# Routing taken out of the queue of second halves, and a norm moved into the scan before it

## The chip, the core and the metric

The kernel runs on one core of a Trainium2 chip. The metric is the device time of one launch in microseconds (us). Engines are called PE (TensorE matmul), PEld (its weight loads), DVE (VectorE), ACT (ScalarE), POOL (GpSimd) and SP (SyncE, which here only issues transfers).

## The reference

One decoder layer over 64 sequences of 128 tokens of width 256, all in float32. It has three parts, each followed by a residual sum and a layer norm:

```python
x = _layernorm(x + mamba(x))            # L0_attn: norm, W_in, conv, silu, selective scan, gate, W_out
x = _layernorm(x + retention(x, ctx))   # L0_xattn: q from x, k and v from ctx, xpos, decay mask
x = _layernorm(x + moe(x))              # L0_ffn: a shared expert, and 2 of 8 routed experts
...
    xn = _layernorm(x, gamma, beta)
    x_inner, z = jnp.split(xn @ W_in, 2, axis=-1)
    x_conv = jax.nn.silu(causal_conv(x_inner))
    xp = x_conv @ W_x                          # B, C (16 states each), delta
    y = _selective_scan(x_conv, A, Bmat, Cmat, softplus(delta))
    return ((y + x_conv * D_skip) * silu(z)) @ W_out + x
...
    probs = sigmoid(x @ router_w.T + routing_bias)
    scores, indices = top_k(probs, 2)          # normed to sum 1
    combined = sum over the two: score * (silu(x @ gate) * (x @ up)) @ down
```

## The kernel before, in words

At run time the kernel picks one of two bodies. With these inputs the decay rows are all alike, so `_shared_decay` runs.

**Groups.** The 64 sequences are 16 groups of 4 (`GB`), so a group has 512 tokens. A group goes through these generators; each `yield` hands control back to a planner, with the number of microseconds of matmul work that should pass before the next step.

- `front` (L632): the norm of x into `xn` (`layernorm`, L577: statistics on DVE, a `pow` on POOL, then `shift` on DVE, then four ACT writes), transposes, the product with `w_in_s`, convolution on DVE (L662), silu, then the products with `w_x_s` for B, C and delta, which go out to DRAM and come back spread over partitions (`bj`, `cj`, `cq`).
- `scan` (L750): the selective scan as matrix products inside each sequence. POOL scales `bj` and `cj` (L754), PE makes sums of the decays (`d`, `dlb`), DVE makes `eq`, `gq` and the mask matrix `mt` (L799), PE transposes `xc` (L806) and multiplies with `mt` (L813), and DVE makes y and the gated `sz` (L817, L820).
- `after` (L824), the second half: product with `w_out_s`, norm, the keys `kh` and values of the context `cT`, queries `qh`, scores, and the second norm, which leaves `x2`.
- `route` (L946): transposes of `x2`, the router's logits, ranks of the experts (`sel`, L985), running counts (`pre`), addresses, and eight indirect stores by POOL (L1028) that scatter the rows of the group to the lists of its experts. For groups in `LATE` (7 to 12) SP then stores `x2` and its transpose as well.
- `early_shared` (L1069): the shared expert, for groups not in `LATE` beside the others, for the rest at the end.

After groups 3, 7, 11 and 15 `tile_list` (L1096) turns the counts into a list of tiles of one expert each. `one_tile` (L1284) does such a tile: its rows and weights are fetched on SP, two products, and an indirect store of the results by POOL.

**The planner.** Several chains run side by side. Each carries a position in units of groups, and the number of microseconds of matmuls until it may go on. `abreast` (L1312) always steps the chain with the lowest position among those that may go on, and jumps its clock ahead when none may. `placed` (L1330) gives a chain its place: `placed(gen, at, length, span)` takes the chain from `at` to `at + span` as `length` microseconds of its own work and waits pass. The chains are: `first_halves` (front and scan of group g from position g-1 on), `second_start` (the same for group 1), `second_halves` (after and route of group g from g+1 on), `shared_ones` (from g+2 on) and `tiles_beside`. What is issued first has priority, but the compiler's scheduler still reorders instructions of an engine where one is ready earlier and its buffer is free.

Gates stand between the chains. The second half of group g begins when g is scanned, and group g-2 has its shared expert added (or, in `LATE`, has been routed). The first half of group g loads the x of g+1 (POOL, L629), and waits until group g-2 has read its x (`read`).

**Buffers.** Most big buffers exist once and are shared by name tags: `xn` and the scan's `eq` are one, `xnT`, `cq` and `xd0` are one, `cT` and `x1T` are one, and so are `qh` and the second copy of the rows to be scattered, `row1`. PSUM has 5 banks `pm` and 3 banks `gu`. Group 1 has buffers of its own in the place of expert weights that are not loaded yet, so that groups 0 and 1 start together.

Of the kernel before, what the change touches and what calls it, by code (L numbers as in the profile page):

```python
# [16 lines left out]
P = 128  # L17
L = 128
D = 256
# [10 lines left out]
GB = 4  # L30
# [481 lines left out]
def _shared_decay(ctx, K):  # L512
# [41 lines left out]
    def buffer(st, shape, name, tag=None):  # L554

        if "own" not in st:
            return one.tile(shape, F32, name=name, tag=tag or name)
        return shaped(st["own"][tag or name], shape)
# [68 lines left out]
    def load_x(g):  # L627
        xt = xts[g % 3]
        nc.gpsimd.dma_start(out=xt, in_=x[g * GB : (g + 1) * GB].rearrange("b l d -> l b d"))  # L629
        return xt  # L630

    def front(st):  # L632


        xt = st["xt"]
        xn = buffer(st, [P, GB, D], "xn", "xn")
        if st is states[0]:
            rstd, shift = K.norm0
            for b in range(GB):
                read_by = nc.scalar.activation(  # L640
                    xn[:, b, :], xt[:, b, :], AF.Identity, bias=shift[:, b : b + 1], scale=rstd[:, b : b + 1]
                )
            first_read.append(read_by.ins.name)
        else:
            yield from layernorm(xn, xt)
        yield 2.6
        xnT = buffer(st, [P, KD, T], "xnT", "xnT")
        transposed(xnT, xn, gam, bet)
        yield 1.2
# [100 lines left out]
    def scan(st):  # L750

        xcf, dl, tok, bj, cj, cq = (st[k] for k in ("xcf", "dl", "tok", "bj", "cj", "cq"))
        for t, h in ((bj, halvesT[0]), (cj, halvesT[1])):
            nc.gpsimd.tensor_tensor(seqs(t), seqs(t), h.unsqueeze(1).to_broadcast([KB, GB, L]), ALU.mult)  # L754

        d1 = little(st, [P, GB, Q], "d1")
        nc.vector.tensor_tensor(
            d1, dl.unsqueeze(2).to_broadcast([P, GB, Q]), place.unsqueeze(1).to_broadcast([P, GB, Q]), ALU.mult
        )
        dlb = little(st, [P, GB, 32], "dlb")  # L760
        nc.vector.tensor_copy(dlb, dl.unsqueeze(2).to_broadcast([P, GB, 32]))
        yield 4.4 if fetched[0] else 2.4
        pin = pm.tile([P, GB, Q], F32, name="pm")
        product(pin.rearrange("p b i -> p (b i)"), lhsT=after_in, rhs=d1.rearrange("p b i -> p (b i)"), start=True, stop=True)
        eq = buffer(st, [P, GB, NS, Q], "eq", "xn")
        nc.vector.tensor_tensor(
            eq, pin.unsqueeze(2).to_broadcast([P, GB, NS, Q]),
            a_row.unsqueeze(1).unsqueeze(3).to_broadcast([P, GB, NS, Q]), ALU.mult,
        )
        pof = pm.tile([KB, T], F32, name="pm")  # L770
        for b in range(GB):
            for q in range(4):
                product(
                    pof[32 * q : 32 * q + 32, b * L : (b + 1) * L], lhsT=dlb[:, b, :], rhs=middle[min(q, 2)],
                    start=True, stop=True, tile_position=(0, 32 * q),
                )
        eb = buffer(st, [KB, T], "eb", "bcs")
        nc.scalar.activation(eb, pof, AF.Exp, scale=a_col)
        nc.scalar.activation(eq, eq, AF.Exp)
        nc.vector.tensor_tensor(bj, bj, eb, ALU.mult)  # L780
        nc.vector.tensor_tensor(cj, cj, eb, ALU.mult)
        yield 4.2
        pmt = pm.tile([P, GB, L], F32, name="pm")
        for b in range(GB):
            product(
                pmt[:, b, :], lhsT=bj[:, b * L : (b + 1) * L], rhs=cj[:, b * L : (b + 1) * L], start=True, stop=True
            )
        nc.vector.tensor_tensor(eq, eq, cq, ALU.mult)
        nc.vector.tensor_tensor(
            eq, eq, tok[:, :, 0:NS].unsqueeze(3).to_broadcast([P, GB, NS, Q]), ALU.mult  # L790
        )
        gq = little(st, [P, GB, Q], "gq")
        nc.vector.tensor_reduce(gq, eq.rearrange("p b n i -> p b i n"), AX.X, ALU.add)
        mt = buffer(st, [P, GB, NQ, Q], "mt", "dm")
        nc.vector.tensor_tensor(
            mt, gq.unsqueeze(2).to_broadcast([P, GB, NQ, Q]), causal.unsqueeze(1).to_broadcast([P, GB, NQ, Q]), ALU.mult
        )
        mtf = mt.rearrange("p b j i -> p b (j i)")
        nc.vector.tensor_tensor(mtf, mtf, pmt, ALU.add)  # L799
        yield  # L800

        xd = [buffer(st, [P, 2, DI], f"xd{j}", tag) for j, tag in enumerate(("xnT", "xd"))]
        for b in range(GB):
            ps = pm.tile([P, DI], F32, name="pm")
            for c in range(CI):
                turn(ps[:, c * P : (c + 1) * P], xcf[:, c, b * L : (b + 1) * L], ident)  # L806
            nc.scalar.activation(xd[b // 2][:, b % 2, :], ps, AF.Copy, scale=dl[:, b : b + 1])  # L807
            yield 0.5 if b < GB - 1 else 3.6
        acc = st["sz"]
        for c in range(CI):  # L810
            ps = pm.tile([P, GB, L], F32, name="pm")
            for b in range(GB):
                product(  # L813
                    ps[:, b, :], lhsT=xd[b // 2][:, b % 2, c * P : (c + 1) * P], rhs=mtf[:, b, :], start=True, stop=True
                )
            y = xcf[:, c, :]
            nc.vector.scalar_tensor_tensor(  # L817
                y, xcf[:, c, :], dsk[:, c : c + 1], ps.rearrange("p b l -> p (b l)"), ALU.mult, ALU.add
            )
            nc.vector.tensor_tensor(acc[:, c, :], acc[:, c, :], y, ALU.mult)  # L820
            yield 0.5 if c < CI - 1 or not fetched[0] else 2.0
        st["acc"] = acc
# [489 lines left out]
    def abreast(*chains):  # L1312

        alive = [[gen, whole, 0.0, 0.0] for gen, whole in chains]
        while any(c[1] for c in alive):
            able = [c for c in alive if c[3] <= work[0]]
            if not able:
                work[0] = min(c[3] for c in alive)  # L1320
                continue
            c = min(able, key=lambda c: c[2])
            try:
                c[2], wait = next(c[0])
            except StopIteration:
                alive.remove(c)
                continue
            c[3] = work[0] + wait

    def placed(gen, at, length, span=1.0):  # L1330

        passed = 0.0
        while True:
            before = work[0]
            try:
                wait = next(gen) or 0.0
            except StopIteration:
                return
            passed += work[0] - before + wait
            yield at + span * min(1.0, passed / length), wait  # L1340
# [2 lines left out]
        yield from front(st)  # L1343
        yield from scan(st)

    def second_half(g, st):
        yield from after(g, st)
        yield 2.6
        yield from route(g, st)
        for k, (groups, *_) in enumerate(BATCHES):  # L1350
            if groups == g + 1:
                tile_list(k)
                refill()
# [142 lines left out]
    def until(ready, at):  # L1496
        while not ready():
            yield at, 0.5

    def first_halves():  # L1500
        states[2]["xt"] = load_x(2)
        yield from placed(start, 0.0, 54.0)
        states[0]["scanned"] = True
        for g in range(2, NG):
            if g + 1 < NG:
                yield from until(lambda: "read" in states[g - 2], g - 1)
                states[g + 1]["xt"] = load_x(g + 1)
            yield from placed(first_half(states[g]), g - 1, 54.0)
            states[g]["scanned"] = True

    def second_start():
        yield from placed(first_half(states[1]), 0.2, 54.0)
        states[1]["scanned"] = True

    def second_halves():
        for g in range(NG):
            yield from until(lambda: "scanned" in states[g] and (g < 2 or "added" in states[g - 2]), g + 1)
            yield from placed(second_half(g, states[g]), g + 1, 60.0)
            states[g]["routed"] = True
            if g in LATE:  # L1520
                states[g]["added"] = True
# [10 lines left out]
    def tiles_beside():  # L1532

        for at, length in places:
            if at >= NG + 1:
                return
            i = listed[0]
            while i == known[0]:
                yield at, 1.0
            yield from placed(one_tile(), at, 11.0, length)  # L1540

    abreast((first_halves(), True), (second_start(), True), (second_halves(), True), (shared_ones(), True), (tiles_beside(), True))
    chains.close()


# [291 lines left out]
```

## Time and profile before

| | |
|---|---|
| median of three runs | 1954.57 us (1946.59 to 1956.8) |
| profiled execution | 1935.52 us, span 1933.7 us |
| mean granted clock of PE | 0.988 |
| PE busy | 1866.0 us, 97% of the span |
| DVE busy | 971.9 us, 50% |
| ACT busy | 748.7 us, 39% |
| POOL busy | 473.1 us, 24% |
| groups 2 to 6 without or with few expert tiles | until about 435 us |
| expert tiles alone | about 1545 to 1790 us |
| last sums and stores | from about 1790 us |

The profile shows one execution. For every engine it has the busy time, and for the waits which instruction ended them. A fraction of the full TensorE clock is shown for each stretch: at 0.50 a matmul takes twice as long. Matmul ends are modelled, so a busy PE can still be below its peak. Line numbers are those of the kernel before.

### The profile page before, as it was taken

How to read it: one execution, taken by the hardware profiler on the slowest of the kernel's cores; microseconds unless marked ns; L12 is line 12 of the kernel's file. 1: busy time of each engine (PE TensorE's matmuls, PEld its weight loads, DVE VectorE, ACT ScalarE, POOL GpSimd, SP SyncE). 2: the span in 40 equal slices, each digit the busy share in tenths (PEclk: the TensorE clock that was granted, in tenths of full speed). 3: DMA queues.
4: the chain of work that ended last, by engine and by line, in shares of the span. 5: the costliest groups of instructions: out<-in, count | busy, mean ns of one | idle time of the engine just before them, and what ended most of it. 6: DMA issues, size and time to landing. Idle time of an engine off the chain costs nothing.

```text
span 1933.7 us, 26599 instructions
## 1 busy us (share of the span) xinstructions
PE 1866.0 (97%) x9252; PEld 1393.1 (72%) x9252; DVE 971.9 (50%) x2409; ACT 748.7 (39%) x1238; POOL 473.1 (24%) x715
## 2 busy tenths in 40 slices
PE   7799999999999998999999999999999999999997
PEld 3656656668686856787877768786877888999554
DVE  5766667745455557455555474554333111111774
ACT  5553553443434343535353544352231222222233
POOL 2102212303030403132322313141313322222111
PEclk9999999999999998999999999999999999999998
DMA  4211211423150214323242224232204443353782
GB/s 142 53 35 44 68 49 41 137 85 95 45 153 28 85 35 153 101 77 113 64 133 93 79 93 123 61 123 92 81 19 128 146 150 118 120 175 107 276 305 89
DMA packets 101352, 199.10 MB, mean 103 GB/s; under 512 B 22904, under 2 KB 61432, under 8 KB 96600
## 3 DMA queue, kind: packets, MB, share of 16 engines
q1 hardware_dynamic: 80952, 144.24, 23.6%
q0 software_dynamic: 17328, 51.41, 7.8%
q10 hardware_dynamic: 2928, 1.65, 0.3%
q8 instruction: 75, 1.23, 0.3%
q14 instruction: 69, 0.57, 0.1%
HBM read 206.81 MB, written 58.08 MB: 137 GB/s over the span
## 4 chain that ended last, share of the span: by engine, by line
PE 72%; DVE 3%; issue 3%; DMA 2%; ACT 2%; POOL 2%; SPq 0%; POOLq 0%; ACTq 0%; DVEq 0%
PE pm L545 37%; PE gu L545 32%; PE pm L549 4%; DMA picked<-ys 1%; POOL rstd L588 1%; DMA ys<-rows_out,to 1%; DVE st L583 0%; DVE x L1305 0%; DMA cq<-chunks 0%; POOL xs L1028 0%; ACT x L593 0%; ACT xn L593 0%; DVE hc L1051 0%; DVE xt L1305 0%; ACT xc L667 0%
## 5 line engine op out<-in xcount | busy, mean ns | idle before, releaser
L545 PE MATMUL gu<-rows_T,routed_gu 128*128 128x256 f32 (+1 forms) x2496 | 499.4, 351 | 1.5 <-ACT rows_T L1232 1.5
L545 PEld LDWEIGHTS gu<-rows_T,routed_gu 128*128 128x128 f32 x2496 | 417.7, 191 | 59.2 <-issue 14.2
L1261 DVE TENSOR_TENSOR hid<-hid,gu 128x512 f32<-128x512 f32 x135 | 92.7, 687 | 394.8 <-PE gu L545 344.4
L545 PE MATMUL pm<-routed_d,hid 128*128 128x256 f32 x1080 | 252.7, 381 | 0.0
L545 PE MATMUL gu<-x2T,shared_w 128*128 128x512 f32 x512 | 232.0, 596 | 4.4 <-DVE hc L1051 3.3
L545 PE MATMUL pm<-xnT,w_in_s 128*128 128x512 f32 x480 | 226.6, 599 | 1.7 <-ACT xnT L606 1.1
L545 PEld LDWEIGHTS pm<-routed_d,hid 128*128 128x128 f32 x1080 | 199.7, 190 | 29.6 <-issue 5.4
L1277 POOL DMA_INDIRECT ys<-rows_out,to x135 | 135.0, 1000 | 331.4 <-ACT rows_out L1276 282.8
L545 PEld LDWEIGHTS gu<-x2T,shared_w 128*128 128x128 f32 x512 | 94.3, 190 | 112.1 <-issue 93.6
L593 ACT ACTIVATE x<-x,shift,rstd 128x256 f32<-128x256 f32 x156 | 82.3, 590 | 232.5 <-DVE shift L590 222.2
L588 POOL TENSOR_TENSOR rstd<-var,mhalf 128x4 f32<-128x4 f32 (+1 forms) x69 | 72.8, 1055 | 370.6 <-DVE var L586 318.6
L662 DVE SCALAR_TENSOR_TENSOR xc<-pm,cw,xc 128x508 f32<-128x508 f32 (+1 forms) x180 | 131.4, 738 | 37.2 <-ACT xc L657 36.0
L545 PEld LDWEIGHTS pm<-xnT,w_in_s 128*128 128x128 f32 x480 | 90.2, 192 | 80.3 <-issue 72.3
L1276 ACT ACTIVATE rows_out<-pm,wt 128x256 f32<-128x256 f32 x135 | 57.9, 471 | 205.2 <-PE pm L545 185.4
L1260 ACT ACTIVATE hid<-gu 128x512 f32<-128x512 f32 x135 | 80.6, 597 | 110.0 <-PE gu L545 109.7
L545 PE MATMUL pm<-w_out_s,sz 128*128 128x256 f32 x512 | 116.4, 381 | 0.4 <-ACT xd L807 0.2
L545 PEld LDWEIGHTS pm<-w_out_s,sz 128*128 128x128 f32 x512 | 95.4, 191 | 14.3 <-issue 1.0
L657 ACT ACTIVATE xc<-pm,cb,cw 128x512 f32<-128x512 f32 x60 | 46.7, 778 | 144.2 <-PE pm L545 144.2
L1028 POOL DMA_INDIRECT xs<-x,index x64 | 71.6, 1118 | 78.0 <-DVE row L1024 42.8
L583 DVE BATCH_NORM_STATS2 st<-x 128x6 f32<-128x256 f32 x196 | 77.4, 408 | 1.6 <-DMA x<-in_x_dram 0.7
L545 PE MATMUL gu<-shared_w,hc 128*128 128x256 f32 x320 | 72.5, 380 | 0.0
L1051 DVE TENSOR_TENSOR hc<-hc,gu 128x512 f32<-128x512 f32 x64 | 43.5, 680 | 55.2 <-PE gu L545 35.1
(288 smaller groups left out, 2571.2 us busy)
## 6 DMA issues: line engine op xcount, KB each, us to landing
routed_gu<-in_ffn_dram SPq DMA_DIRECT2D x78, 1024.0 KB
routed_d<-in_ffn_dram SPq DMA_DIRECT2D x78, 512.0 KB
picked<-ys SPq DMA_DIRECT2D x16, 1024.0 KB
rows_in<-xs SPq DMA_DIRECT2D x57, 258.0 KB
cT<-in_ctxT_dram POOLq DMA_DIRECT2D x16, 512.0 KB, 4.1
x_rows<-x SPq DMA_DIRECT2D x16, 512.0 KB
cq<-chunks SPq DMA_DIRECT2D x15, 512.0 KB
x<-in_x_dram POOLq DMA_DIRECT2D x9, 512.0 KB, 4.2
```

Source lines behind the costliest of these rows:

```text
L545: nc.tensor.matmul(out, lhsT=lhsT, rhs=rhs, **how)
L549: nc.tensor.transpose(out, src, ident)
L583: nc.vector.bn_stats(st, src[:, b, :])
L588: nc.gpsimd.tensor_tensor(rstd, var, mhalf[:, 0:n], ALU.pow)
L593: nc.scalar.activation(dst[:, b, :], src[:, b, :], AF.Identity, bias=shift[:, b : b + 1], scale=rstd[:, b : b + 1])
L657: nc.scalar.activation(xcf[:, c, :], ps, AF.Identity, bias=cb[:, c : c + 1], scale=cw[:, c, TAPS - 1 : TAPS],)
L662: nc.vector.scalar_tensor_tensor(xc[:, c, :, s:], ps3[:, :, : L - s], cw[:, c, TAPS - 1 - s : TAPS - s], xc[:, c, :, s:], ALU.mult, ALU.add,)
L1028: s = nc.gpsimd.indirect_dma_start(out=xs, in_=rows[k][:, b, :], in_offset=None, out_offset=bass.IndirectOffsetOnAxis(ap=index[:, b, k : k ...
L1260: nc.scalar.activation(hc, psg, AF.Silu)
L1261: nc.vector.tensor_tensor(hc, hc, psu, ALU.mult)
L1276: nc.scalar.activation(y[:, j, :], ps[:, j, :], AF.Copy, scale=wt[:, j : j + 1])
L1277: s = nc.gpsimd.indirect_dma_start(out=ys, in_=y[:, j, :], in_offset=None, out_offset=bass.IndirectOffsetOnAxis(ap=to[:, j : j + 1], axis=0),)
```

## The change

It has two parts. In the first, `scan` of group 0 and of every group from 2 on makes the norm of the next group of `first_halves` (group 2 after group 0, else g+1): statistics, `pow` and `shift` right after `mt`, and the four ACT writes into `xn` after the transposes of `xc`. `front` of that group finds `xn` made and skips its norm and the planned waits of 4.2 and 2.6 behind it. In the second, `route` and the tile lists leave `second_halves` and become a chain `routings` of their own. `after` of group g now goes from g+1 to g+1.6, `routing` of group g from g+1.6 to g+2, and the second half of the next group no longer has to wait for the routing of this one.

```diff
--- before.py
+++ after.py
@@ -633,8 +633,14 @@
 
 
         xt = st["xt"]
-        xn = buffer(st, [P, GB, D], "xn", "xn")
-        if st is states[0]:
+        made = "xn" in st
+        if made:
+            xn = st["xn"]
+        else:
+            xn = buffer(st, [P, GB, D], "xn", "xn")
+        if made:
+            pass
+        elif st is states[0]:
             rstd, shift = K.norm0
             for b in range(GB):
                 read_by = nc.scalar.activation(
@@ -643,7 +649,7 @@
             first_read.append(read_by.ins.name)
         else:
             yield from layernorm(xn, xt)
-        yield 2.6
+        yield 0.0 if made else 2.6
         xnT = buffer(st, [P, KD, T], "xnT", "xnT")
         transposed(xnT, xn, gam, bet)
         yield 1.2
@@ -797,6 +803,13 @@
         )
         mtf = mt.rearrange("p b j i -> p b (j i)")
         nc.vector.tensor_tensor(mtf, mtf, pmt, ALU.add)
+
+        norm = None
+        if "next" in st:
+            then = st["next"]
+            xn = then["xn"] = buffer(then, [P, GB, D], "xn", "xn")
+            norm = layernorm(xn, then["xt"])
+            next(norm)
         yield
 
         xd = [buffer(st, [P, 2, DI], f"xd{j}", tag) for j, tag in enumerate(("xnT", "xd"))]
@@ -806,6 +819,8 @@
                 turn(ps[:, c * P : (c + 1) * P], xcf[:, c, b * L : (b + 1) * L], ident)
             nc.scalar.activation(xd[b // 2][:, b % 2, :], ps, AF.Copy, scale=dl[:, b : b + 1])
             yield 0.5 if b < GB - 1 else 3.6
+        for _ in norm or ():
+            pass
         acc = st["sz"]
         for c in range(CI):
             ps = pm.tile([P, GB, L], F32, name="pm")
@@ -1343,9 +1358,7 @@
         yield from front(st)
         yield from scan(st)
 
-    def second_half(g, st):
-        yield from after(g, st)
-        yield 2.6
+    def routing(g, st):
         yield from route(g, st)
         for k, (groups, *_) in enumerate(BATCHES):
             if groups == g + 1:
@@ -1499,6 +1512,8 @@
 
     def first_halves():
         states[2]["xt"] = load_x(2)
+        for g in (0, *range(2, NG - 1)):
+            states[g]["next"] = states[max(g + 1, 2)]
         yield from placed(start, 0.0, 54.0)
         states[0]["scanned"] = True
         for g in range(2, NG):
@@ -1513,9 +1528,16 @@
         states[1]["scanned"] = True
 
     def second_halves():
+
         for g in range(NG):
             yield from until(lambda: "scanned" in states[g] and (g < 2 or "added" in states[g - 2]), g + 1)
-            yield from placed(second_half(g, states[g]), g + 1, 60.0)
+            yield from placed(after(g, states[g]), g + 1, 38.0, 0.6)
+
+    def routings():
+        for g in range(NG):
+            yield from until(lambda: "x2" in states[g], g + 1.6)
+            yield g + 1.6, 2.6
+            yield from placed(routing(g, states[g]), g + 1.6, 26.0, 0.4)
             states[g]["routed"] = True
             if g in LATE:
                 states[g]["added"] = True
@@ -1539,7 +1561,7 @@
                 yield at, 1.0
             yield from placed(one_tile(), at, 11.0, length)
 
-    abreast((first_halves(), True), (second_start(), True), (second_halves(), True), (shared_ones(), True), (tiles_beside(), True))
+    abreast((first_halves(), True), (second_start(), True), (second_halves(), True), (routings(), True), (shared_ones(), True), (tiles_beside(), True))
     chains.close()
 
 
```

## The prediction

> **What bounds the kernel now.** I read, in this order, the page's busy shares and slices, the PE's waits, the PE's own timeline in the stretches where it waits, the granted clock in windows around those, and the POOL and DVE timelines of one group.
>
> ```profile
> PE 1866.0 (97%) x9252; PEld 1393.1 (72%) x9252; DVE 971.9 (50%) x2409; ACT 748.7 (39%) x1238; POOL 473.1 (24%) x715
> ...
> PE   7799999999999998999999999999999999999997
> ...
> PEclk9999999999999998999999999999999999999998
> ```
>
> The first row says that TensorE is busy for all but 1933.7 - 1866.0 = 67.7 us. The change touches no matmul, so nothing but this idle time and the time lost to a lowered clock can be won. The slices show where it lies: at the start, at the end, and in one slice in the middle (the sixteenth, 8 in both rows). By windows: 13.9 us idle before 48 us, about 24 us from 48 to 435 us, nothing from 435 to 720 us, 8.0 us from 725 to 773 us, about 3 us from there to 1545 us, and 18 us after 1790 us. The end (late sums, loads of picked rows) is not touched.
>
> ```profile
> PE pm L549 <- ACT xn L593: 8.8, 10, 2.0
> ...
> PE pm L545 <- DVE cj L781: 4.6, 3, 2.3
> PE pm L545 <- DVE sel L985: 4.5, 2, 2.8
> ...
> PE pm L545 <- DVE dlb L761: 3.1, 2, 2.9
> ```
>
> Columns: total us, times, longest. The largest wait is for `xn`, the norm at the head of the first half; `sel` is the router's. Two single rows of the PE timeline, one of each kind (the bracket is the idle time before it):
>
> ```profile
> 141.50 0.63 PE L545 MATMUL pm<-sel,upto 128*128 128x32 f32 x2 [2.78 <-DVE sel L985]
> ```
> ```profile
> 313.43 0.33 PE L549 MATMUL pm<-ident,xn 128*128 128x128 f32 x1 [1.48 <-ACT xn L593]
> ```
>
> And the gap in the middle, where group 7 is routed beside group 9's scan:
>
> ```profile
> 724.52 0.38 PE L549 MATMUL pm<-ident,bcs 128*128 128x128 f32 x2
> 726.67 0.41 PE L545 MATMUL pm<-sel,upto 128*128 128x32 f32 x2 [1.77 <-DVE sel L985]
> 727.36 0.41 PE L545 MATMUL pm<-pre,ones 128*128 128x32 f32 x2 [0.28 <-DVE pre L991]
> 730.63 0.66 PE L545 MATMUL pm<-d,after_in 128*128 128x64 f32 x2 [2.86 <-DVE dlb L761]
> 731.22 1.94 PE L545 MATMUL pm<-middle,dlb 128*32 128x128 f32 x32
> 735.47 2.04 PE L545 MATMUL pm<-cj,bj 128*128 128x128 f32 x8 [2.31 <-DVE cj L781]
> ```
> ```profile
> 725.00:730.00 5.00, 0.82 (x4) 0.59 (x4) 4.71 (x25) 3.18 (x5) 1.26 (x1) 0.78 0.53 177
> 730.00:735.00 5.00, 2.52 (x34) 1.89 (x34) 3.30 (x13) 1.63 (x2) 2.60 (x3) 0.50 0.48 138
> 735.00:740.00 5.00, 4.54 (x21) 4.57 (x22) 4.08 (x4) 1.37 (x2) 4.08 (x4) 0.50 0.23 82
> ```
>
> Columns of the windows: us, busy PE, PEld, DVE, ACT, POOL, granted clock, DMA share, GB/s. The clock drops to 0.50 after the gap, so what the PE then does takes twice its time: the gap costs more than itself.
>
> **The norm moved (edit 1).** Removed from the head of `front`: the layernorm call and the planner's waits of 4.2 and 2.6; added in `scan` of the group before: the same instructions. They are 4 bn_stats (0.40 us), 4 aggregates (0.17), `var`, `shift` (0.16 each) on DVE, one `pow` (1.05) on POOL and four ACT writes (2.08 together). No DMA moves: the load of x is still issued one group ahead (301.71 us for a norm that would now come some 60 us later; 4.2 us to landing), past nothing new. Group 0 prepares group 2, then each its next; group 1 keeps its own norm.
>
> What goes: the PE's waits for `xn` by its timeline are 2.02 (group 2), 1.23, 1.63, 1.64 and 2.15 us (group 6), 8.7 in all. After group 6 tiles of the experts hide the norm already, and there I cost the gain at nothing. Two of the gaps carried the clock down: 0.56 and 0.87 in the 3 us windows from 96 and 99 us (3 x 0.44 + 3 x 0.13 = 1.7 us), 0.50 and 0.95 from 390 and 393 us (1.5 + 0.15 = 1.65 us). At most 8.7 + 1.7 + 1.65 = 12.0 us.
>
> Here the Trainium skill speaks another way. "TensorE: Matmul & The Clock Gate", Part 1, says that the clock falls to half after an idle window of about 3.4 us; by it no gap of 2 us costs clock, and the edit would bring 8.7 us. The rows show 0.56 after a gap of 2.02 us (with a 0.3 to 0.5 us trickle of work behind it). I take the rows, 12.0.
>
> What it may cost: the DVE work is the same in sum, but now comes in one step with `mt`, ahead of the four y updates (0.74 + 0.69 us each) that free the PSUM banks. From 291 to 313 us DVE idles only about 3 us, so 4 x (0.32 + 0.09) + 0.3 = 1.9 us put first are 1.9 us late for what follows. In the trace of before, the stats of xt stood in the same stretch (304.17 to 311.22 us), behind the y updates; they leave there what they take earlier. Bounds: nothing, if they slip into DVE's idle time before the scan (263 to 275 us is nearly empty), or 1.9 us in each of the five groups without tiles, 9.5 us. I take 3 us, nearer the lower end, as five PSUM banks stand between. ACT is idle from 292 to 305 us, where its four writes would go: nothing; without that hole they would hold the next evacuation 2.1 us.
>
> **Routing as its own chain (edit 2).** Routing no longer stands in the queue of second halves: `after(g+1)` need not wait for `route(g)` and its planned waits (1.0 + 0.6 + 2.2 + 4.6 or 7.6 + 0.4 + 3.0 + 5.0 + 5.0). The positions hardly move: attention's own length is 21.6 of matmuls plus 12 of waits, some 34; 34/60 = 0.57 before and 0.6 x 34/38 = 0.54 now, routing starts at 0.60 both times and ends near 1.0. So the order stays where chains are plentiful, and only where all others wait can `after(g+1)` step in. It is still gated: it needs group g+1 scanned, and group g-1's shared expert added. Two places qualify.
>
> At 141.5 us (group 0 routed, no gate for group 1): 2.78 us of gap, and the clock at 0.50 for 141 to 147 us and 0.91 for the next three, (2.5 + 3.0) x 0.5 + 0.27 = 3.0 us. In all 5.8. The DVE is full there (3.00 of 3.00 us from 138 to 141 us), so I take half, 2.9.
>
> At 724.9 us: group 6's shared expert has just ended (724.5 us), group 8 is scanned, and its w_out products follow only at 741.0 us behind the tile list: 2 x 3.6 us of matmuls that depend on nothing still running. The gaps are 1.77 + 0.28 + 2.86 + 2.31 = 7.2 us; the clock costs 0.82 x 0.22 + 2.52 x 0.5 + 4.54 x 0.5 + 5.0 x 0.15 (0.85 from 740 us) = 4.5 us. Together 11.7. What is late next: the work drawn forward is missing at 741 to 763 us, before the first tile, but the next first half, ready without its norm, has 14 us of w_in products for that. I take 8 us.
>
> The queues that routing is moved past: on POOL its 8 indirect stores, 0.96 + 0.30 us each:
>
> ```profile
> 297.34 0.96 POOL L1028 DMA_INDIRECT xs<-row,index  x1 [0.30 <-issue]
> 301.71 0.81 POOL L629 DMA_DIRECT2D x<-in_x_dram  x1 [3.42 <-DVE x L841]
> 304.35 1.05 POOL L588 TENSOR_TENSOR rstd<-var,mhalf 128x4 f32<-128x4 f32 x1 [1.82 <-DVE var L586]
> ```
>
> They run from 287.09 to 298.30 us; the attention's `pow` comes 6 us after the last. On SP: two stores of x2 for groups 7 to 12 and the fetches behind the tile list; attention issues nothing on SP, so no order changes there. `row1` lies in the place of `qh`, so the next `qh` (DVE, some 316 us) waits for the last of these stores (298.3 + 2.6 to landing = 301): 15 us of slack, which an earlier attention eats into. The load of cT, on POOL, is issued 55 us before its use (318.9 for 374 us). Cost between nothing and one scatter row, 10 us, in each of the two places; I take 1 us each, as before the slack was 6 and 15 us.
>
> **Sum.** 12.0 - 3.0 + 2.9 + 8.0 - 2.0 = 17.9, say 18 us. The profiled execution took 1935.5 us (span 1933.7), and would take 1917.5, 0.93% less. The median of the three runs, 1954.6, stands 1.0% above the profiled one; 0.93% off it is 1936.4 us.
>
> **Rivals.**
> *Hidden anyway (same).* Other waits take the place of the `xn` ones: each group still shows 0.8 us for `mt`, and `xnT` and the y updates now follow each other closely. If those give back the 8.7 us and the gap at 725 us stays since `after(8)` isn't let in, 3 us remain: 1951 us. For it: PE waits of 0.2 to 0.8 us stand everywhere behind the larger ones. Against: from 415 us on the PE idles nowhere, whenever it has a choice of work.
>
> *The early norm caught behind the stores (slower).* The `shift` of the norm sits in DVE's in-order queue right after `mt`, and waits for a `pow` in POOL's queue. The 8 stores of routing take 10.1 us there. In before `mt` came at 294.4 us, inside their run of 287 to 298 us. If the `pow` comes behind the stores, DVE stands up to 10 us with the y updates, the residuals and the experts' products queued behind it. Taking 4 us of stall (half a row left, less a little) in 13 groups, 52 us, of which half comes through to the PE past its five banks, 26 us, against some 12 won: 14 slower, 1969 us. It decides from about 2 us of stall in each group (13 us on the PE). Against: by position the norm (0.65 of the group) precedes the stores (0.83), and the stats can go early. For: the planner counts matmuls, not POOL's microseconds.
>
> *All of it (faster still).* Everything above at its full size, 12.0 + 5.8 + 11.7 = 29.5 us: 1925 us.
>
> *It doesn't do what it says:* for group 1 it surely doesn't; for the others the norm may be drawn ahead or held, but the head of `front` loses its wait either way.
>
> **How the numbers follow.** About 0.5% (10 us) is what a measurement can tell from no change. My sum and "all of it" have 0.56 together (0.46 and 0.10), hidden anyway 0.23, caught behind the stores 0.21. The likeliest case alone spans 1925 to 1944. The range goes on to 1968: half the slower case, and 1920 below for a little beyond the full size; some 0.17 are left out.
>
> **What would show it.** Right: the wait PE <- ACT `xn` is gone or under 1 us; w_out products of group 8 stand between 725 and 735 us and the clock stays at 1.00 there; 50 to 435 us loses 10 us or more of idle time; the end is as before. Wrong: `shift` waiting on POOL for well over its present 61.7 us in total (0.93 each), with PE waits for `xc` (L817) or `xnT` new in the list; or the gap of the sixteenth slice still there.

## The result and the profile after

The changed kernel takes 1960.22 us (median of 20 runs, 1955.83 to 1964.78), the kernel before 1948.70 us (20 runs, 1944.93 to 1958.89): a ratio of 1.0054 with the interval [1.0044, 1.0065]. It is slower by 0.54%, some 10.5 us by the ratio, where 0.93% faster was forecast. The two profiled executions stand further apart, 1935.52 and 1962.05 us, since the one of before was among its fastest. So times are compared by ratios below, each against runs of the kernel before on the same chip, and the traces are read for where waits stand, not for the last microseconds.

The page of the changed kernel, its first two parts:

```profile
PE 1874.3 (96%) x9252; PEld 1400.2 (71%) x9252; DVE 985.4 (50%) x2409; ACT 761.6 (39%) x1248; POOL 466.0 (24%) x715
...
PE   7889998899999998999999999999999999999997
...
PEclk9899999899999998999999999999999999999998
```

The span is 1960.3 us. The number of matmuls is unchanged, but PE now idles 1960.3 - 1874.3 = 86.0 us (67.7 before), and is busy 8.3 us longer for the same work: that is lowered clock (mean 0.982, 0.988 before). The slices show new dips near the start: the third, seventh and eighth in the row of PE, the second and eighth in that of the clock. What PE waits for (total us, times, longest):

```profile
PE pm L545 <- DVE qh L875: 12.0, 2, 7.0
PE pm L545 <- DVE dlb L767: 10.6, 2, 7.6
...
PE pm L549 <- ACT xn L646: 5.5, 1, 5.5
PE pm L545 <- DVE cj L787: 5.3, 2, 3.1
PE pm L545 <- ACT xnT L606: 4.8, 3, 2.1
```

The waits for the norm of later groups (ACT `xn`, L593 before, 8.8 us in 10) are gone; L646 is the first group's own start, as long as it was before. But `qh` is new, and `dlb` and `xnT` have grown (3.1 and 1.1 us before). Two rows of DVE's waits go with them:

```profile
DVE shift L590 <- POOL rstd L588: 92.7, 65, 5.8
...
DVE qh L873 <- DMA xs<-row,index: 12.1, 2, 7.4
```

and the first of these in the kernel before:

```profile
DVE shift L590 <- POOL rstd L588: 61.7, 66, 2.4
```

The `shift` of the norms waits 31 us more in all for POOL's `pow`. A wait of about 1 us is the `pow` itself; 18 of the 65 waits are now longer than 1.6 us, where 2 of 66 were. And `qh`, which lies in the place of `row1`, now waits for routing's last stores, which it never did in the trace of before.

Most of the new idle time lies early. The stretch from 50 to 440 us, first after, then before (us, busy PE, PEld, DVE, ACT, POOL, granted clock, DMA share, GB/s):

```profile
50.00:440.00 390.00, 352.46 (x1742) 239.42 (x1740) 250.81 (x614) 171.01 (x262) 71.23 (x79) 0.94 0.21 62
```
```profile
50.00:440.00 390.00, 365.51 (x1805) 243.53 (x1805) 262.84 (x639) 184.22 (x279) 79.11 (x83) 0.97 0.21 64
```

PE idles 37.5 us there instead of 24.5, at a lower clock, where at least 10 us less was to be seen. The gap at 725 us, in the same columns:

```profile
725.00:730.00 5.00, 5.00 (x21) 3.66 (x20) 3.58 (x12) 2.23 (x2) 1.52 (x2) 1.00 0.08 26
730.00:735.00 5.00, 5.00 (x20) 3.52 (x19) 0.14 (x2) 1.47 (x3) 3.78 (x5) 1.00 0.58 206
735.00:740.00 5.00, 5.00 (x21) 3.79 (x20) 0.65 (x2) 0.60 (x1) 2.41 (x3) 1.00 0.24 87
...
765.00:770.00 5.00, 2.44 (x21) 2.04 (x19) 5.00 (x7) 2.53 (x4) 1.17 (x3) 0.93 0.96 375
770.00:775.00 5.00, 3.31 (x14) 3.06 (x14) 2.92 (x4) 2.08 (x4) 0.00 (x0) 0.50 0.48 165
```

It is closed, at full clock, as forecast, but not by the work that was forecast. Products of the shared expert, of the next first half and of expert tiles fill it; the w_out products of group 8 come only behind it:

```profile
736.36 3.62 PE L545 MATMUL pm<-w_out_s,sz 128*128 128x256 f32 x16
```

A new gap stands 40 us later, where PE waits for `qh` (3.3 us) and the clock is 0.50 again.

### The profile page after: what moved, and what is told of

Read it like the earlier page. It is cut to its first block, busy times and chain, and to the rows that moved or that the text cites. A ratio compares the mean times of both kernels' runs of the same rounds, so it can differ in the third digit from the quotient of the medians.

```text
span 1960.3 us, 26607 instructions
## 1 busy us (share of the span) xinstructions
PE 1874.3 (96%) x9252; PEld 1400.2 (71%) x9252; DVE 985.4 (50%) x2409; ACT 761.6 (39%) x1248; POOL 466.0 (24%) x715
## 5 line engine op out<-in xcount | busy, mean ns | idle before, releaser
L545 PEld LDWEIGHTS pm<-routed_d,hid 128*128 128x128 f32 x1080 | 202.0, 192 | 35.3 <-issue 10.3
L593 ACT ACTIVATE x<-x,shift,rstd 128x256 f32<-128x256 f32 x156 | 82.8, 591 | 115.2 <-DVE shift L590 112.0
L1043 POOL DMA_INDIRECT xs<-x,index x64 | 63.6, 993 | 121.0 <-DVE row L1039 83.9
L1247 ACT COPY rows_T<-pm 128x512 f32<-128x512 f32 (+1 forms) x78 | 41.1, 528 | 123.2 <-PE pm L549 95.6
```

The costliest lines, as they stand in the source:

```text
L545: nc.tensor.matmul(out, lhsT=lhsT, rhs=rhs, **how)
L593: nc.scalar.activation(dst[:, b, :], src[:, b, :], AF.Identity, bias=shift[:, b : b + 1], scale=rstd[:, b : b + 1])
L1043: s = nc.gpsimd.indirect_dma_start(out=xs, in_=rows[k][:, b, :], in_offset=None, out_offset=bass.IndirectOffsetOnAxis(ap=index[:, b, k : k ...
```

## The experiments

The kernels are arranged by the question that they answer. Where an expectation gives theories letters, a letter stands for the cause that is named with it. Every ratio is to the kernel before on the same chip.

### Each part alone

**The early norm alone**: routing goes back into the queue of second halves.

```diff
-    def routing(g, st):
+    def second_half(g, st):
+        yield from after(g, st)
+        yield 2.6
         yield from route(g, st)
...
-            yield from placed(after(g, states[g]), g + 1, 38.0, 0.6)
-
-    def routings():
-        for g in range(NG):
-            yield from until(lambda: "x2" in states[g], g + 1.6)
-            yield g + 1.6, 2.6
-            yield from placed(routing(g, states[g]), g + 1.6, 26.0, 0.4)
+            yield from placed(second_half(g, states[g]), g + 1, 60.0)
...
```

> The early norm alone; routing stays in the queue of second halves. Theory A (the routing chain is what costs: the next attention runs into routing's row1 and its late stores): 5 to 12 us below the kernel before (1937 to 1944), no PE wait for xn after group 1, and PE waits for qh under 1 us. Theory B (the early norm costs, by DVE work ahead of the y updates and shift behind other POOL work): 5 to 15 us above before, with PE waits behind dlb, xnT or xc. Theory C (only the changed order of the matmuls and the clock after gaps count, either edit does it): within 5 us of before.

Measured: 1975.99 us, a ratio of 1.0155 [1.0142, 1.0168]. The part that was to win is the one that costs most. PE's longest list entry is now

```profile
PE pm L545 <- ACT xnT L606: 24.3, 8, 5.3
```

and one of the eight waits can be followed through four engines. The timelines of POOL, DVE, ACT and PE in the same 15 us (start, us, engine, line, operation, and in the bracket the idle time before it and its releaser):

```profile
157.20 0.96 POOL L1043 DMA_INDIRECT xs<-row,index  x1 [0.31 <-issue]
158.46 0.96 POOL L1043 DMA_INDIRECT xs<-row,index  x1 [0.30 <-issue]
159.42 0.82 POOL L629 DMA_DIRECT2D x<-in_x_dram  x1
160.25 1.08 POOL L588 TENSOR_TENSOR rstd<-var,mhalf 128x4 f32<-128x4 f32 x1
```
```profile
156.03 0.17 DVE L586 TENSOR_SCALAR var<-mv 128x4 f32<-128x4 f32 x1
156.11 0.68 DVE L873 TENSOR_TENSOR kh<-pm,rot_s 128x512 f32<-128x512 f32 x1
161.37 0.16 DVE L590 SCALAR_TENSOR_TENSOR shift<-mv,rstd 128x4 f32<-128x4 f32 x1 [4.58 <-POOL rstd L588]
```
```profile
161.57 1.58 ACT L593 ACTIVATE x<-x,shift,rstd 128x256 f32<-128x256 f32 x3 [16.42 <-DVE shift L590]
163.06 1.42 ACT L606 ACTIVATE xnT<-pm,bet,gam 128x512 f32<-128x512 f32 x2
```
```profile
158.41 1.02 PE L545 MATMUL gu<-x2T,shared_w 128*128 128x512 f32 x2
163.87 3.78 PE L545 MATMUL pm<-xnT,w_in_s 128*128 128x512 f32 x4 [4.44 <-ACT xnT L606]
```

`var` is ready at 156.2 us, but its `pow` stands behind the last of routing's eight stores (149.42 to 159.42 us) and a load, and starts at 160.25. DVE's queue stops at `shift` for 4.58 us. ACT's queue stops at the three writes of x1 that need `shift`, and the evacuation `xnT`, which needs nothing of this norm, stands behind them. PE waits 4.44 us for `xnT`, and then its four matmuls take 3.78 us, where four of the same take 1.88 us at 172.15 us: the granted clock is 0.50 from 164 to 168 us. The same meeting comes four times between 160 and 410 us. DVE stalls 4.58, 4.50, 4.51 and 4.03 us in them, and PE waits 4.44, 4.36, 4.37 and 5.27 us, 18.4 of the 24.3 us. The norm that is caught is not the early one. It is the norm of x1 in the second half that runs beside it.

**Routing as its own chain alone**: the early norm is dropped, so that `front` makes its norm and waits as before.

```diff
-        for g in (0, *range(2, NG - 1)):
-            states[g]["next"] = states[max(g + 1, 2)]
```

> Routing as its own chain alone; every norm stays at the head of front. Theory A: 10 to 20 us above before (1959 to 1969), since the xn waits of 8 us are back as well, with PE waits for qh of 5 us or more. Theory B: 3 to 12 us below before, the gap at 725 us filled. Theory C: 0 to 10 us above.

Measured: 1949.29 us, 1.0019 [1.0012, 1.0026]: a small loss, where 8.9 us were to be won. Two windows of this kernel, the columns as above:

```profile
660.00:800.00 140.00, 132.76 (x715) 100.80 (x714) 90.42 (x241) 63.52 (x103) 34.76 (x47) 0.98 0.36 110
800.00:1460.00 660.00, 644.23 (x3264) 492.05 (x3263) 347.82 (x821) 273.70 (x447) 167.58 (x229) 1.00 0.27 85
```

and the same two of the kernel before:

```profile
660.00:800.00 140.00, 131.80 (x600) 92.23 (x599) 84.97 (x216) 54.85 (x89) 28.86 (x37) 0.95 0.25 84
800.00:1460.00 660.00, 656.95 (x3385) 511.83 (x3384) 338.47 (x843) 269.58 (x448) 174.59 (x239) 1.00 0.29 90
```

The first stretch holds the routing of group 7 and what follows it in both kernels. Here that routing comes 30 us earlier (`sel` at 696 us instead of 726), and its gap comes with it: PE idles 5.7 us between 695 and 710 us. Over the whole stretch the chain saves 132.76 - 131.80 = 1.0 us of idle time and, by the clock of 0.98 instead of 0.95, some 4 us more, where 8.0 were forecast. In the second, in which the trace of before had nearly no idle time, PE loses 656.95 - 644.23 = 12.7 us. There attention of one group, routing of another and expert tiles now overlap, and a `pow` meets other work on POOL. One such meeting, in three lines of POOL, one of DVE and one of PE:

```profile
860.64 1.04 POOL L1292 DMA_INDIRECT ys<-rows_out,to  x1 [0.15 <-issue]
861.99 0.97 POOL L1292 DMA_INDIRECT ys<-rows_out,to  x1 [0.30 <-issue]
862.99 1.05 POOL L588 TENSOR_TENSOR rstd<-var,mhalf 128x4 f32<-128x4 f32 x1
```
```profile
864.07 1.23 DVE L590 SCALAR_TENSOR_TENSOR shift<-mv,rstd 128x4 f32<-128x4 f32 x1 [4.69 <-POOL rstd L588]
```
```profile
865.70 0.43 PE L545 MATMUL pm<-d,after_in 128*128 128x64 f32 x2 [1.11 <-DVE d L763]
```

`shift` again, this time behind the scaling of `bj` and two stores of tile results; the scan's `d` stands behind it in DVE's queue, and PE waits for that.

### What of the early norm costs: the norm, the waits, or POOL

**The early norm with the planned waits kept**: the norm is made in the scan, and `front` still lets the planner count 4.2 and 2.6 us of matmuls before its transposes.

```diff
         if made:
-            pass
+            yield 4.2
...
-        yield 0.0 if made else 2.6
+        yield 2.6
```

> The early norm alone, but front keeps the planner's waits of 4.2 and 2.6 us that the edit had taken out, though nothing is left to wait for; instructions as in the early norm alone (1976 us). Theory D (the loss is the lost lead: with 6.8 us of planned waits gone, each first half runs that much ahead, so the second half's norm meets routing's eight stores on POOL): the waits for xnT of 4.4 us go, and the time falls by 20 to 30 us, to within 5 us of before. Theory B (the norm's own work on DVE and ACT at its new place): still 20 us or more above before.

Measured: 1920.46 us, 0.9924 [0.9911, 0.9937]. The same norm in the same place, and with two waits of the planner put back a gain of 0.76% stands where a loss of 1.55% was. PE idles 58.0 us (span 1917.2, busy 1859.2) instead of 96.0, the clock is 0.990 instead of 0.981. The waits of DVE and the place on POOL that answers to the one above:

```profile
DVE shift L590 <- POOL rstd L588: 59.0, 65, 2.6
```
```profile
155.65 0.96 POOL L1043 DMA_INDIRECT xs<-row,index  x1 [0.30 <-issue]
156.63 0.81 POOL L629 DMA_DIRECT2D x<-in_x_dram  x1
157.62 1.04 POOL L588 TENSOR_TENSOR rstd<-var,mhalf 128x4 f32<-128x4 f32 x1 [0.19 <-DVE var L586]
```

The `pow` still comes right after stores and load, but now POOL waits 0.19 us for `var`: the norm comes just after the stores, where without the waits it came 4 us too early. The planned waits did not only bridge the norm. They also set how far the first half runs ahead of routing, and with it where the second half's norm falls.

**Half of the waits kept**: only 3.4 of the 6.8 us.

```diff
-        yield 0.0 if made else 2.6
+        yield 3.4 if made else 2.6
```

> The early norm alone with a planned wait of 3.4 us at the head of front: half of the 6.8 us kept. If the loss grows with the lead: between the kernels with all and with none of it, ratio 1.000 to 1.008. If it is a collision that either happens or not: near 0.992 or near 1.015.

Measured: 1.007 [1.0052, 1.0087] (1963.57 us). `shift` waits 69.5 us, the longest 4.4; `xnT` 5.0 us in 5. It lies between 0.9924 and 1.0155 in time and in waits, but the single stall is not smaller. Of the four early stalls of `shift` one is left, at 163.59 us and 4.43 us long; the other three are gone, and two of 3.5 and 3.7 us stand in other places. A meeting happens or it does not, and half the lead brings fewer of them. PE's waits for `xnT` explain only 3.9 of the 28 us between 0.9924 and 1.007; where the rest comes from was not traced.

**The root of the x1 norm off POOL**: the early norm alone once more, without planned waits; only the `pow` of the norm of x1 is replaced, by a root on ACT and a reciprocal on DVE.

```diff
-        nc.gpsimd.tensor_tensor(rstd, var, mhalf[:, 0:n], ALU.pow)
+        if root:
+            nc.scalar.activation(rstd, var, AF.Sqrt)
+            nc.vector.reciprocal(rstd, rstd)
+        else:
+            nc.gpsimd.tensor_tensor(rstd, var, mhalf[:, 0:n], ALU.pow)
...
-        norm = layernorm(x1, x1)
+        norm = layernorm(x1, x1, True)
```

> The early norm alone, with the first norm of the second half (x1) no longer on POOL: a square root on ACT and a reciprocal on DVE. If the 4.4 us waits for xnT come from this norm's pow behind the eight stores: DVE's 4.5 us waits for shift go there, the xnT waits fall under 1.5 us each in groups 3 to 6, 12 to 25 us less, 1951 to 1964. ACT pays a table load or two of 1.28 us in each group. If ACT or DVE hold xnT for other reasons: no change beyond 5 us.

Measured: 1932.27 us, 0.998 [0.9971, 0.9988]. No step of any chain is moved, one instruction of 1.05 us in each group leaves POOL's queue, and the kernel gains 1.75 points of the 2.31 between the two kernels above. PE's waits for `xnT` fall from 24.3 to 1.1 us. At the place followed above PE has the same products in the same order, without the wait. One thing besides POOL differs there: ACT now takes `xnT` first, at 160.63 us, and the writes of x1 after it. So the run does not part the late `pow` from the place of `xnT` behind x1's writes; it shows what the two cost together. PE still waits 10.4 us once for `dlb`, near 130 us, a gap that the kernel with planned waits does not have.

**The same replacement in the kernel before**, as a control.

> Control: the kernel before with the same square root on ACT for x1. There this pow stands 6 us behind the last store, so nothing is to be won: within 5 us of before, or up to 5 us above it by the table loads.

Measured: 0.9997 [0.9989, 1.0005]. And with the norm of x2 off POOL as well:

> Control: the kernel before with both norms of the second half off POOL. If they help only where they meet the stores: a ratio of 0.998 to 1.002. If a norm off POOL is worth something by itself (DVE's 61.7 us of waits for shift halved): 0.994 to 0.998.

Measured: 0.9989 [0.9976, 1.0003]. DVE's waits for `shift` fall from 61.7 to 32.5 us in this second control, and the time does not follow. So a norm without POOL is worth nothing in the kernel before that these runs can tell, and the total of the `shift` waits is no price in time.

### What the chain costs on top

**The change with the planned waits kept.** The edit is that of the early norm with the planned waits kept.

> The changed kernel with the same planned waits of 4.2 and 2.6 us kept at the head of front. Theory D: the 12 us of waits for qh and the xnT waits go, and it falls to about the time of the routing chain alone (1949 us) or below it by the 8 us of xn waits, 1941 to 1950. Theory B: within 4 us of the changed kernel.

Measured: 1.0033 [1.0021, 1.0046] (1942.61 us). With the waits kept in both, the chain costs 1.0033 - 0.9924 = 1.1 points, 21 us. Against the changed kernel, though, the waits bring back only 1.0054 - 1.0033 = 0.2 points, hardly more than the intervals can tell. The long waits for `qh` and `dlb` go as Theory D had it (PE idles 19.7 us from 50 to 440 us, 37.5 in the changed kernel), but from 800 to 1460 us PE is busy 646.03 us instead of 650.62: the loss moves to where the chain alone has it. `shift` waits 87.4 us. Its three longest waits, 5.3, 5.0 and 6.0 us near 860, 956 and 1054 us, stand behind the scaling of `bj` and two stores of tile results, as in the chain alone, and not behind routing's stores.

**The same, and the second half of a group waits until the group before is routed**, so that routing no longer overlaps attention.

```diff
-            yield from until(lambda: "scanned" in states[g] and (g < 2 or "added" in states[g - 2]), g + 1)
+            yield from until(lambda: "scanned" in states[g] and (g < 2 or "added" in states[g - 2]) and (g < 1 or "routed" in states[g - 1]), g + 1)
```

> The changed kernel with the planned waits kept, and the second half of each group waiting until the group before it has been routed, so that the routing chain has its own positions but runs beside no second half, as before. If the overlap of routing with the next attention costs the 21 us between the two kernels with waits kept (ratios 1.0033 and 0.9924): the ratio falls to 0.991 to 0.995. If it is the new positions and the order of the chains: it stays at 1.000 or above.

Measured: 0.9938 [0.992, 0.9955] (1936.02 us). The line of DVE's waits falls back:

```profile
DVE shift L590 <- POOL rstd L588: 58.7, 65, 2.8
```

With the waits kept, then, the overlap itself, which the edit was made to allow, is what the chain costs: 1.0033 - 0.9938 = 1.0 points.

**Only the first overlap taken away**: in the changed kernel, group 1's second half waits for the routing of group 0.

```diff
-            yield from until(lambda: "scanned" in states[g] and (g < 2 or "added" in states[g - 2]), g + 1)
+            yield from until(lambda: "scanned" in states[g] and (g < 2 or "added" in states[g - 2]) and (g != 1 or "routed" in states[0]), g + 1)
```

> The changed kernel, but the second half of group 1 waits until group 0 has been routed, as before the change. If letting it in at 119 us, ahead of group 0's routing and shared expert, makes the gap of 7.6 us behind dlb at 122 to 130 us: that gap goes or shrinks under 3 us, 4 to 8 us less (1952 to 1956). If the gap comes from the early norms on DVE and POOL alone: it stays, and the time within 2 us of the changed kernel.

Measured: 1.0095 [1.0079, 1.0111]. The wait for `dlb` stays (10.3 us, once), so letting this second half in early isn't what makes it; the early norm alone shows it too (9.8 us), and the one with planned waits doesn't. `qh` (15.9) and `xnT` (12.8) get worse. The gate changed other waits than the one that it was set for.

**Routing's stores in the other order**, the rows of `row1` first, so that the next `qh` finds their place free 5 us sooner.

```diff
-        for k in range(2):
+        for k in (1, 0):
```

> The changed kernel, but the four stores of row1 are issued ahead of the four of x2, so row1 (which lies in the place of qh) comes free about 4 x 1.27 = 5 us earlier. If the 12 us of PE waits for qh, and the half clock after them, are behind these stores: they fall from 7.0 and 5.0 us to 2 us and nothing, 10 us less of idle time and 3 to 5 us of clock, 1946 to 1952 us. If the stores don't matter (other DVE work holds qh): unchanged within 3 us.

Measured: 1.0093 [1.0077, 1.0108], slower still. PE's wait for `qh` L875 goes (12.0 to 3.0 us), but the other four rows are read in place, and the one who waits for those is now late:

```profile
DVE x L1016 <- DMA xs<-x,index: 41.9, 5, 9.3
```

(29.4 us before the swap), with `xnT` 8.6 and `x` 6.7 us new or larger on PE.

**Both norms off POOL in the changed kernel.** The edit as above, for x1 and x2.

> The changed kernel with both norms of the second half (x1 and x2) taken off POOL: square root on ACT, reciprocal on DVE. If DVE's waits for shift behind other POOL work (92.7 us in total, against 61.7 before) are what the changed kernel loses by: 10 to 20 us below it, a ratio to before of 0.995 to 1.000. If row1 in the place of qh is the larger part (12 us of PE waits and the half clock behind them): the ratio stays between 1.001 and 1.006, and the qh waits are still there.

Measured: 0.9958 [0.9942, 0.9974] (1939.88 us), from 1.0054. `shift` waits 41.7 us, PE's waits for `xnT` fall from 4.8 to 0.7 us, and from 800 to 1460 us PE is busy 659.35 us instead of 650.62. The waits for `qh` stay:

```profile
PE pm L545 <- DVE qh L879: 12.7, 2, 6.8
```

**The same with the stores swapped.**

> The changed kernel with both norms of the second half off POOL (ratio 0.9958, 12.7 us of PE waits for qh left), and row1's four stores issued first. If row1 in the place of qh costs what its waits show: the qh waits fall under 5 us and the ratio to 0.987 to 0.992. If the waits are only exchanged for others, as with the swap alone: 0.994 to 0.998.

Measured: 1.0036 [1.0023, 1.0049]. The row shown above falls from 12.7 to 2.0 us, but a neighbouring row of `qh` (L880) comes with 4.8, so that all waits for `qh` go from 16.5 to 11.5 us. From 50 to 440 us PE wins 362.20 - 356.76 = 5.4 us, and from 800 to 1460 us it loses 659.35 - 645.73 = 13.6 us. The swap exchanges one reader that waits for another, so it doesn't isolate `qh`; that share stays open. A buffer of its own for `row1` would isolate it, and was not tried.

### The best version

**The early norm with planned waits, routing in its old queue, both norms off POOL.**

> The early norm with the planned waits kept (ratio 0.9924), and both norms of the second half off POOL. DVE's waits for shift are 59.0 us in total there, none over 2.6 us, so little is left to be won: a ratio of 0.989 to 0.994; above 0.997 if the table loads on ACT cost.

Measured: 1927.81 us, 0.9895 [0.9877, 0.9912]. It beats both kernels. The `shift` waits are 24.2 us in all, the longest 1.2. The interval overlaps that of the early norm with waits alone (0.9924 [0.9911, 0.9937]) by a hair's breadth, 0.9911 to 0.9912, and they ran on different chips; that the norms off POOL add 0.3% here is likely, not shown.

## Why the prediction was wrong

The ratios in one table (the columns: the next group's norm where it was, early with planned waits, early without them):

| | norm as before | early, waits kept | early, waits removed |
|---|---|---|---|
| routing in its queue | 1 | 0.9924 | 1.0155 |
| routing a chain | 1.0019 | 1.0033 | 1.0054 |

**The step that failed.** Two terms of the sum failed, and both are about the same slack, that of the second half's norms in POOL's queue.

The first is the planned waits. The prediction says of edit 1: "Removed from the head of `front`: the layernorm call and the planner's waits of 4.2 and 2.6", and then costs the norm's instructions only. Removing the waits was costed at nothing. By the upper row it costs 1.0155 - 0.9924 = 2.3 points, 45 us, five times the 9 us that the forecast had the norm bring. They kept a planned distance of 6.8 us between a first half and routing, and without it the `pow` of x1 comes beside routing's stores.

The second is "I take 1 us each, as before the slack was 6 and 15 us", for the stores against the `pow` and for `row1` in the place of `qh`. In the changed kernel, taking the `pow` of the second half's two norms off POOL is worth 1.0054 - 0.9958 = 0.96 points, 19 us, and the same in the kernel before is worth 0.1, with nothing inside its interval. So one part of a term that stands at 2.0 us in the sum measures some 19 us. It was also drawn too narrow: in the changed kernel the long waits of `shift` stand behind routing's stores in some groups (5.8 us at 174.89, 4.4 us at 1330.94), and in others behind the scaling of `bj` and `cj` and stores of tile results (4.5 us at 1098.63), which the prediction did not count. A slack of 6 us and a removed lead of 6.8 us were both written down and not put side by side.

Either loss of order is enough by itself to take the gain away. By the lower row, putting the waits back brings only 0.2 points, since the overlap of routing with the next attention takes the slack too. With the overlap gated away as well, the ratio is 0.9938. From 0.9958 to the forecast of 0.9907 there are 0.5 points more, 10 us. The waits for `qh` that stand there, 12.7 us, are of this size, but no run shows that they are the rest.

**The rival had the mechanism, and the wrong victim.** "Caught behind the stores" described `shift` in DVE's queue behind a `pow` behind eight stores, gave 2 us of stall as the point from which it decides, and 1969 us. The early norm alone shows this path, with 4.0 to 4.6 us of stall and 4.4 to 5.3 us on PE in each of four places. But it named the early norm, and put against itself that this norm precedes the stores by position. It does; the norm in attention is the one that follows. It also let half of DVE's stall come through by way of y and the banks. In the four places nearly all of it came through, and the way was ACT's queue: x1's writes, and `xnT` behind them. In the changed kernel this way carries less (4.8 us for `xnT`), and `qh` and `dlb` carry more.

**The slack of `qh`.** It was 15 us before, and the changed kernel waits 12 us of PE for `qh`. The slack was a property of the very order that the edit gives up. Here is `qh` at its worst, on POOL, DVE and PE:

```profile
305.32 0.96 POOL L1043 DMA_INDIRECT xs<-row,index  x1 [0.30 <-issue]
```
```profile
308.24 0.69 DVE L873 TENSOR_TENSOR qh<-pm,rot_s 128x512 f32<-128x512 f32 x1 [4.72 <-DMA xs<-row,index]
```
```profile
310.28 0.77 PE L545 MATMUL pm<-qh,kh 128*128 128x128 f32 x2 [6.97 <-DVE qh L875]
```

The last store is issued until 306.28 us, and `qh` starts at 308.24 when it has landed; 6.97 us of PE are lost. The clock of the next 2 us windows is 0.50, 0.50 and 0.66.

**"The order stays where chains are plentiful".** It did not: from 800 to 1460 us, where the forecast had no cost and no gain, the chain alone loses 12.7 us and the changed kernel 656.95 - 650.62 = 6.3 us. The gain was looked for in the two places with idle time. The loss sat in part where there was none yet, and for the changed kernel in larger part (13.0 us) before 440 us, just where the waits for `xn` had gone.

**What was right.** The waits for `xn` went, and the early norm is worth 0.76% or 15 us where the order around it is kept; the forecast was 12.0 - 3.0 = 9. PE's idle time from 50 to 440 us falls to 15.2 us there, by 9.3 us, where the waits for `xn` were 8.7. That y and the residuals come late behind the norm, costed at 3 us, shows in no PE wait of that kernel: neither `sz` nor `x` of L856 is in the list. The gap at 725 us closes at clock 1.00, but the w_out products of group 8 do not stand in it, and with routing alone the gap only moves: that part of the mechanism was not right. The end is unchanged (354.94 us busy from 1540 to 1900 us, 355.59 before). `shift` "waiting on POOL for well over its present 61.7 us" was named as what would show the forecast wrong, and it did, with `xnT` in the list.

**The two edits together.** Their losses do not add: 1.0155 and 1.0019 give 1.0054. It may be that a routing of its own also moves its stores away from where the shortened first half puts the `pow`. This reading fits the waits (PE for `xnT` 4.8 us instead of 24.3), but no run tells it from other shifts of the order.

## What to carry to other kernels

A planned wait that seems to cover one latency may also hold two chains apart: before taking it out, lay its length beside every slack that it could eat, above all on a queue that carries both long transfers and a short instruction of a critical chain. Follow a short instruction through all the queues behind it; here 1 us on POOL, come late, stops DVE, then ACT, then PE, and PE at work that needs nothing of it. To find out whether such a meeting is the cause, take the small instruction to another engine, and do the same in the kernel before as a control.

## What the runs showed of the hardware

- **A lowered clock comes late and outlasts the gap.** In the changed kernel PE stops at 1045.96 us for 2.10 us. In windows of 2 us:

```profile
1046.00:1048.00 2.00, 0.00 (x0) 0.00 (x0) 1.97 (x4) 2.00 (x5) 0.00 (x0) 1.00 0.85 231
1048.00:1050.00 2.00, 1.94 (x4) 1.01 (x5) 1.54 (x3) 0.67 (x2) 0.00 (x0) 0.81 0.95 393
1050.00:1052.00 2.00, 2.00 (x5) 1.21 (x5) 0.42 (x1) 0.78 (x1) 0.00 (x0) 0.50 0.06 21
1052.00:1054.00 2.00, 2.00 (x8) 1.43 (x7) 1.80 (x3) 0.00 (x0) 0.00 (x0) 0.84 0.00 0
```

  The clock is full during the gap and falls only when work is back. In windows of 0.5 us it is 1.00 or 0.50 in all but the two at the edges. So a mean of 0.81 puts the fall 0.8 us before 1050, at 1049.2 us, 3.2 us after PE stopped, and 0.84 puts the return 0.6 us after 1052. It is low for 0.8 + 2.0 + 0.6 = 3.4 us and loses 1.7 us more. The Trainium skill, in "TensorE: Matmul & The Clock Gate", Part 1, has the clock go to half after an idle window of about 3.4 us and back after a busy one of that length. The length of the low stretch agrees. The idle window does not: PE was idle for 2.10 us only, and the 3.4 us before the fall hold 1.3 us of matmuls (until 1045.96 and from 1048.06 us).
- **Eight indirect stores hold POOL for 10 us** (149.42 to 159.42 us in the early norm alone), 0.96 to 1.11 us each and 0.30 between, and a `pow` of 128 x 4 behind them, 1.05 us by itself, starts 4 us after its input is ready. Two stores of tile results hold it likewise (860.64 to 862.96 us in the chain alone).
- **One instruction in each group, of 1.05 us on POOL, was worth 34 us** in a kernel whose POOL is busy for 24% of the span (a ratio of 0.998 without it there, against 1.0155), with ACT's order changed at the same time.
